# A graph network stack whose run checks its own lists: the check moved beside layer 3, d added by VectorE, ln_b added earlier, and VectorE counted at 0.9 by the planner

## The chip, the cores and the metric

The kernel runs on one core of one Trainium2 chip. The metric is device time in microseconds, as the median of several runs; lower is better. A core has TensorE (PE in the profile; PEld is its weight load), VectorE (DVE), ScalarE (ACT), GpSimd (POOL) and SyncE (SP). Each engine works through its own queue of instructions in order and waits on semaphores for the others. SP issues the plain DMAs, POOL the gathers (indirect DMAs).

## The reference

4096 nodes with 128 features, and a dense 4096 x 4096 adjacency `adj` of which few entries are not zero. There are four layers, each with `h = relu(layernorm(x))` and `x = x + layer(h, adj)`:

```python
# layer 0: h @ W_self.T + (adj @ h) @ W_neigh.T + b
# layer 1: Chebyshev terms: h @ w0 + (adj @ h) @ w1 + (2 * adj @ (adj @ h) - h) @ w2 + bias
# layer 2: attention over the columns of adj, weights exp(leaky_relu(src + dst)) times adj, normalised
# layer 3:
s = node_feats @ msg_w[:, :D].T
d = node_feats @ msg_w[:, D:].T
messages = gelu(s[:, None, :] + d[None, :, :] + msg_b)
aggregated = einsum('ijd,ij->id', messages, adj)
new_feats = concatenate([node_feats, aggregated], -1) @ upd_w.T + upd_b
h = gelu(new_feats) + node_feats
return (h - mean(h)) / sqrt(var(h) + eps) * ln_w + ln_b
```

Only pairs (i, j) with a nonzero entry of `adj` need a message in layer 3.

## The kernel before

The nodes are reordered by their expected degree, which is fixed at build time. The kernel scans `adj` once and builds lists on the chip: of the columns that each stripe of 256 rows needs, and of the single entries of each block of 128 rows. The lengths of all lists are fixed beforehand from the expected degrees with a margin. In the end the kernel looks whether a list has overflowed: `n_bad` is the number of partitions with an overflow. It is loaded into a register of every engine (L1648), and `tc.If(some_bad > 0)` (L1655) runs a dense version, which these inputs never need.

**Stages.** The scan with layer 0 lies between 0 and about 410 us of the profiled span, layers 1 and 2 of the products (both multiplications of the Chebyshev layer) up to about 870, attention up to about 1185, and layer 3 behind it, its start beside the last columns of attention.

**The planner.** The order of all instructions is made while the program is built, by the class `Plan` (L255). Each piece of work is a generator that yields what it wants next: an engine with a duration, a buffer of a pool (`Slots`), or an `Event`. The planner keeps a clock for each engine and serves the piece that can begin first, a lower rank before a higher one within a short patience. What a piece emits after its turn is appended to the program; `in_order` (L348) fixes that order on each engine. So durations that the planner books don't change an instruction, they change the order in which all are issued. `on_dve(n)` books 0.16 + 1.05e-3 n us for VectorE, and PE durations are multiplied by `PE_TIME` (0.72). Where the plan has a gap on PE, `fill` (L604) emits matmuls on a tile of zeros (L609) into an idle bank.

**Layer 3** is the class `Messages` (L1316). It works in eight groups of four blocks of rows. There are 158 chunks of up to 128 list entries, taken in 49 batches of up to four. `d` lies in DRAM (`d_tab`, written at L1307). For each group:

- `prepare` (L1354) computes s for its rows, adds `msg_b` (L1369), makes the diagonal's messages (`own`: add at L1374, GELU at L1376, times the diagonal `r` of L1380, into the accumulator at L1385).
- `message` (L1391), one for each batch: ACT and VectorE build a selection matrix (`mt` at L622, `msel` at L624); VectorE builds `r`, which places the entries' values (L1400); POOL has gathered the rows of `d` into `m` (L553); PE adds in PSUM `ident` times `m` (L1406) and the selected rows of s (L1408); ACT takes the GELU from PSUM back into `m` (L1412); PE multiplies into the accumulator (L1418). The buffers of `m` are four own tiles and halves of attention's e and tau tiles, hence those names in the profile.
- `finish` (L1425) copies the accumulator (L1430), multiplies by the update weights (L597), adds `upd_b` (L1438), GELU (L1441), adds h and takes the mean (L1444 to L1446), squares (L1450), square root (L1453), reciprocal (L1455, L1456), normalises (L1459), multiplies by ln_w (L1463), adds ln_b (L1464) and x (L1465), and stores (L1467).

PSUM has three accumulators, three banks and two "picks", which become banks in layer 3. There are one, later four, lanes for selections and two, later four, tiles `r`. [...]

**The check** (L1621 to L1646) stands after `plan.run()` (L1618), so behind everything on VectorE: 67 comparisons of one element per partition, 12 small operations, one matmul over the partitions (L1644) and a copy to integers (L1646).

Of the kernel before, what the change touches and what calls it, by code (L numbers as in the profile page):

```python
# [254 lines left out]
class Plan:  # L255
# [8 lines left out]
    BYTES = 330e3  # L264
    TABLE = 1.3
    PATIENCE = 0.3
    PE_TIME = 0.72
    FILLED = 0.8
    SHORT = 0.8
# [29 lines left out]
    def run(self, until=lambda: False):  # L299
        while self.tasks and not until():  # L300
            able = []
            for task in list(self.tasks):
                while isinstance(task.want, Event) and task.want.time is not None:
                    if task.want.time + self.HOP > task.ready:
                        task.ready, task.engine = max(task.ready, task.want.time), None
                    self._next(task)
                want = task.want
                if want is None or isinstance(want, Event):
                    continue
                if isinstance(want, Slots):  # L310
                    if not want.free:
                        continue
                    begin = max(task.ready, min(want.free)[0])
                else:
                    begin = max(task.ready + self.HOP * (task.engine != want[0]), self.free[want[0]])
                able.append((begin, task.rank, task.serial, task))
            assert able, [(t.generator.__name__, t.want) for t in self.tasks]
            first = min(able)
            want = first[3].want
            if not isinstance(want, Slots):  # L320

                first = min((a[1:] for a in able if a[0] <= first[0] + min(self.PATIENCE, want[1]) and
                             not isinstance(a[3].want, Slots) and a[3].want[0] == want[0]))
                first = next(a for a in able if a[3] is first[2])
            begin, task = first[0], first[3]
            want = task.want
            if isinstance(want, Slots):
                first = min(want.free)
                want.free.remove(first)
                task.ready = begin  # L330
                self._next(task, want.items[first[1]])
                continue
            duration = want[1]
            if want[0] == "PE":
                duration *= self.PE_TIME
                gap = begin - self.free["PE"]
                if self.filler and gap > self.SHORT:
                    self.filler(self.free["PE"], gap * self.FILLED)
            self.finish = begin + duration
            if len(want) > 2 and want[2] != self.table:  # L340
                self.table = want[2]
                self.finish += self.TABLE
            self.free[want[0]] = self.finish
            task.ready, task.engine = self.finish, want[0]
            self._next(task)
# [33 lines left out]
def sparse_stack(tc, x, adj, adjT, diag, w_self, w_neigh, b0, w1, b1, w2, att_src, att_dst,  # L379
# [10 lines left out]
    with ExitStack() as ctx:  # L390
# [21 lines left out]
        def by_block(v, n):  # L412

            return v[:, None, :].to_broadcast([P, n, D])
# [188 lines left out]

        def fill(begin, time):  # L604

            idle = min((free, i, slots.items) for slots in (banks, picks) for free, i in slots.free + [(1e9, 0)])
            if idle[0] < begin - 1.0:
                for _ in range(int(time / 0.22)):
                    nc.tensor.matmul(idle[2][idle[1]], nothing[:, :P], nothing, start=True, stop=True)  # L609
# [706 lines left out]
        class Messages:  # L1316
# [37 lines left out]
            def prepare(self, g):  # L1354
# [32 lines left out]
                plan.release(owns, own)  # L1387
                plan.release(r_tiles, r)
                self.s_here[g].set(plan.finish)

            def message(self, g, b, u, c, chunks, m, here):  # L1391
                n = len(chunks)
                yield u_done[u.number]
                lane = yield m_lanes
                yield from selection(lane, mids[:, u.number, :], half[:, u.number:u.number + 1], c, n)
                yield self.s_here[g]
                r = yield r_tiles
                yield "DVE", 0.35 * n
                for q, k in enumerate(chunks):
                    nc.vector.tensor_scalar(r[:, q, :], iota_row[:, :P], e_row[:, k:k + 1], e_val[:, k:k + 1],  # L1400
                                            op0=ALU.is_equal, op1=ALU.mult)
                for q in range(n):
                    yield here[q]
                p = yield banks
                yield "PE", n * 0.84
                nc.tensor.matmul(p[:, :n * D], ident, m[:, :n, :], start=True, stop=False)  # L1406
                for q in range(n):
                    nc.tensor.matmul(p[:, q * D:(q + 1) * D], lane["sel"][:, q, :], self.s_rows[g][:, b % GB, :],  # L1408
                                     start=False, stop=q == n - 1)
                plan.release(m_lanes, lane)  # L1410
                yield on_act(n * D, "gelu")
                nc.scalar.activation(m[:, :n, :], rows_of(p, n), AF.Gelu)  # L1412
                plan.release(banks, p)
                yield "PE", 0.42 * n
                acc = self.acc[g]
                for q in range(n):
                    self.left[b] -= 1
                    nc.tensor.matmul(acc[:, b % GB * P:(b % GB + 1) * P], m[:, q, :], r[:, q, :], start=False,  # L1418
                                     stop=all(self.left[g * GB + k] == 0 for k in range(GB)))
                plan.release(r_tiles, r)  # L1420
                plan.release(messages, m)
                if all(self.left[g * GB + k] == 0 for k in range(GB)):
                    plan.start(self.finish(g), -2)

            def finish(self, g):  # L1425
# [33 lines left out]
                    nc.scalar.activation(f[:, k, :], f[:, k, :], AF.Identity, scale=st[:, 2, k:k + 1],  # L1459
                                         bias=st[:, 3, k:k + 1])  # L1460
                plan.release(stats, st)
                yield "DVE", 2.1
                nc.vector.tensor_mul(f, f, by_block(ln_w_sb, GB))  # L1463
                nc.vector.tensor_add(f, f, by_block(ln_b_sb, GB))  # L1464
                nc.vector.tensor_add(f, f, xN[:, blocks, :])  # L1465
                yield SP
                nc.sync.dma_start(out_rows[:, blocks, :], f)  # L1467
# [18 lines left out]
            plan.release(banks, p)  # L1486

        w02, w22, w2T, dst_w = (kept(k, (P, D)) for k in ("w02", "w22", "w2T", "dst_w"))


        making = ctx.enter_context(ExitStack())
# [112 lines left out]
        with tc.tile_pool(name="lm", bufs=1, reuse_waits="tile") as lm:  # L1604
# [10 lines left out]
            more_of(m_lanes, message_lanes(lm, range(1, 4)))  # L1615
            more_of(banks, [picks.items[i] for _, i in picks.free])
            picks.free = []
            plan.run()  # L1618


            bad = lm.tile([P, NPAIR + NU + 2], F32, name="bad", tag="bad")  # L1621
            for i, item in enumerate(ROWS + COLS):
                nc.vector.tensor_scalar(bad[:, i:i + 1], pair_total[:, i:i + 1], float(item.cap * P), None, op0=ALU.is_gt)
            for i, u in enumerate(UNITS):
                nc.vector.tensor_scalar(bad[:, NPAIR + i:NPAIR + i + 1], total[:, i:i + 1], float(u.places), None,
                                        op0=ALU.is_gt)
            nc.vector.tensor_reduce(bad[:, NPAIR + NU:NPAIR + NU + 1], over, axis=AX.X, op=ALU.max)

            count = lm.tile([P, NB], F32, name="count", tag="count")
            found = lm.tile([P, NB], F32, name="found", tag="found")  # L1630
            hub = sum(u.block == 0 for u in UNITS)
            nc.vector.tensor_reduce(count, marks.rearrange("p (b h) -> p b h", h=2), axis=AX.X, op=ALU.add)
            nc.vector.tensor_scalar(count, count, 2.0, float(-N), op0=ALU.mult, op1=ALU.add)
            nc.vector.tensor_scalar(found, diag_sb, 0.0, None, op0=ALU.is_gt)
            nc.vector.tensor_sub(count, count, found)
            nc.vector.tensor_reduce(found[:, 0:1], deg[:, :hub], axis=AX.X, op=ALU.add)
            nc.vector.tensor_copy(found[:, 1:], deg[:, hub:])
            nc.vector.tensor_tensor(count, count, found, op=ALU.not_equal)
            nc.vector.tensor_reduce(bad[:, NPAIR + NU + 1:], count, axis=AX.X, op=ALU.max)
            worst = lm.tile([P, 2], F32, name="worst", tag="worst")  # L1640
            nc.vector.tensor_reduce(worst[:, 0:1], bad, axis=AX.X, op=ALU.max)
            nc.vector.tensor_scalar(worst[:, 1:2], worst[:, 0:1], 0.0, None, op0=ALU.is_gt)
            p = accs.items[0]
            nc.tensor.matmul(p[:, :1], ones, worst[:, 1:2], start=True, stop=True)  # L1644
            n_bad = kept("n_bad", (P, 1), I32)
            nc.vector.tensor_copy(n_bad, p[:, :1])  # L1646
        in_order(tc)
        return nc.values_load(n_bad[0:1, 0:1], min_val=0, max_val=P)  # L1648

# [337 lines left out]
```

## Time and profile before

| what | value |
|---|---|
| runs | 1197.93 us median of three (1197.63, 1197.93, 1202.9) |
| profiled execution | 1500.43 us, of which the span from first to last instruction is 1498.6 us |
| mean granted clock of TensorE | 0.834 |
| gathers of layer 3 (L553 from d_tab) | 158, 0.95 us each, one every 1.25 us |
| ident matmuls of layer 3 (L1406) | 46.2 us busy |
| last store issued (L1467) | 1474.62 us |
| check on VectorE (L1623 to L1646) | 1474.5 to 1481.4 us |

The profiled execution is 302.5 us longer than the median of the runs, so a position in the span is not one in a run. A profile line for an instruction group has line, engine, operation, tiles, count, duration, and the idle time before it with what ended that. "remote" and "another core or an unknown queue" are waits whose end the profile can't name, "issue" is time in which an engine waited for nothing that it shows. Lines of the sequencers (SPq, POOLq and so on) show loads into registers, branches, drains and semaphores, which are not counted as busy.

### The profile page before, as it was taken

Reading aid. Unit: us, or ns where it says so; the run is one execution under the profiler, and the core shown is the slowest. Engines: PE = TensorE matmul, PEld = TensorE weight load, DVE = VectorE, ACT = ScalarE, POOL = GpSimd, SP = SyncE. Lnnn points to the kernel's source line nnn. Section 1 sums busy time; section 2 is a strip of 40 time slices with the busy share of each in tenths; the row PEclk is TensorE's granted clock in tenths of the full one; section 3 lists DMA queues with packets and bytes.
Section 4 is the critical chain, followed back from the end, with each engine's and each line's share of the span. In section 5 each row is a group of like instructions: output and inputs, shape, how many; then the busy total and the mean of one; then the engine's idle time right before and its main releaser. Section 6 shows DMA issues by size and latency. Waiting matters only on the chain.

```text
span 1498.6 us, 19187 instructions
## 1 busy us (share of the span) xinstructions
PE 1058.5 (71%) x5943; PEld 723.0 (48%) x5943; DVE 791.5 (53%) x2982; ACT 670.3 (45%) x1344; POOL 767.3 (51%) x832
## 2 busy tenths in 40 slices
PE   6786788887477867467774289668777955668880
PEld 3454555554256556355653255334444633556660
DVE  5796666886366566355663156334343612344453
ACT  5983666663121212114452087546564801236462
POOL 4135754544455656635667527726576165654500
PEclk9897898888697888677897599879897986888885
DMA  8999999994366778666542045313333121121200
GB/s 252 352 338 318 335 308 342 341 310 145 92 194 191 205 217 232 171 193 176 156 132 80 22 123 146 108 39 87 107 101 97 41 59 43 47 51 48 67 17 17
DMA packets 175415, 236.03 MB, mean 157 GB/s; under 512 B 22452, under 2 KB 155336, under 8 KB 167112
## 3 DMA queue, kind: packets, MB, share of 16 engines
q1 hardware_dynamic: 148904, 186.45, 37.6%
q0 software_dynamic: 26400, 48.27, 13.1%
q8 instruction: 49, 0.80, 0.2%
q14 instruction: 62, 0.51, 0.1%
HBM read 203.41 MB, written 31.23 MB: 157 GB/s over the span
## 4 chain that ended last, share of the span: by engine, by line
PE 26%; issue 11%; ACT 9%; another core or an unknown queue 8%; DVE 5%; DMA 1%; SPq 0%; ACTq 0%; DVEq 0%
PE acc L1254 4%; PE acc L1252 4%; PE bank L597 3%; PE acc L1138 3%; PE acc L1155 2%; PE acc L1418 2%; PE pick L609 1%; PE bank L1406 1%; PE bank L1408 1%; ACT e L1228 1%; ACT junk L1450 1%; ACT e L1231 1%; ACT junk L568 1%; PE pick L1418 1%
## 5 line engine op out<-in xcount | busy, mean ns | idle before, releaser
L553 POOL DMA_INDIRECT e_val<-in_adj,e_at x158 | 155.5, 984 | 48.0 <-issue 46.5
L553 POOL DMA_INDIRECT g<-h_tab,fetch_row x136 | 135.7, 998 | 73.1 <-issue 34.3
L609 PE MATMUL pick<-nothing 128*128 128x512 f16 x532 | 141.4, 413 | 2.4 <-issue 2.4
L1138 PE MATMUL acc<-big,hA 128*128 128x256 f32 x448 | 124.6, 422 | 16.3 <-DMA big<-in_adjT 7.3
L609 PEld LDWEIGHTS <-nothing 128*128 128x128 f16 x795 | 83.5, 108 | 102.7 <-issue 38.3
L553 POOL DMA_INDIRECT g<-a_tab,fetch_col x74 | 77.7, 1049 | 92.5 <-issue 43.6
L553 POOL DMA_INDIRECT rseg<-in_adjT,seg_row x68 | 71.3, 1048 | 94.3 <-issue 39.7
L1138 PEld LDWEIGHTS acc<-big,hA 128*128 128x128 f32 x448 | 90.6, 213 | 32.8 <-DMA big<-in_adjT 8.8
L553 POOL DMA_INDIRECT cseg<-in_adj,seg_col x74 | 70.8, 957 | 66.2 <-DVE pcum L634 23.5
L553 POOL DMA_INDIRECT g<-u_tab,fetch_row x68 | 64.7, 951 | 63.7 <-PE acc L1155 32.5
L890 DVE SCALAR_TENSOR_TENSOR ehit<-ehit,pos,pick 128x32 f32<-128x32 f32 (+7 forms) x158 | 38.8, 285 | 108.0 <-issue 64.6
L1235 DVE TENSOR_TENSOR tau<-e,big 128x512 f32<-128x512 f32 (+3 forms) x61 | 54.2, 889 | 70.2 <-ACT e L1231 43.7
L887 ACT COPY ehit<-pick 128x192 f32<-128x192 f32 (+7 forms) x74 | 20.4, 286 | 157.8 <-remote 72.5
L553 POOL DMA_INDIRECT tau<-d_tab,e_col x63 | 60.5, 961 | 56.2 <-PE acc L1418 15.1
L553 POOL DMA_INDIRECT m<-d_tab,e_col x70 | 68.0, 972 | 38.0 <-issue 16.5
L768 ACT ACTIVATE mask<-dst 128x2048 fp8e4<-128x2048 f32 x43 | 81.8, 1903 | 12.1 <-DMA dst<-in_adj 9.5
L1155 PE MATMUL acc<-big,g 128*128 128x256 f32 x272 | 80.8, 437 | 2.7 <-DMA big<-r_tab 1.9
L622 ACT ACTIVATE sel_t<-iota_row,mids 128x512 f32<-128x512 f32 (+3 forms) x43 | 27.1, 642 | 118.1 <-DVE mids L617 69.8
L568 ACT ACTIVATE junk<-xN,stat 128x128 f32<-128x128 f32 x128 | 51.4, 401 | 60.7 <-DVE stat L564 23.1
L609 PE MATMUL bank<-nothing 128*128 128x512 f16 x263 | 74.8, 430 | 1.6 <-DVE s L1369 1.2
L883 PE MATMUL pick<-eA,esel 128*128 128x65 f16 (+7 forms) x158 | 27.3, 249 | 61.4 <-DVE esel L624 24.1
L1138 PE MATMUL acc<-big,hB 128*128 128x256 f32 x224 | 64.2, 428 | 0.0
(328 smaller groups left out, 2727.5 us busy)
## 6 DMA issues: line engine op xcount, KB each, us to landing
dst<-in_adj SPq DMA_DIRECT2D x43, 1024.0 KB
big<-in_adjT SPq DMA_DIRECT2D x45, 512.0 KB
raw<-in_adj SPq DMA_DIRECT2D x21, 1024.0 KB
big<-in_adjT SPq DMA_DIRECT2D x66, 256.0 KB
big<-r_tab SPq DMA_DIRECT2D x30, 512.0 KB
c_tab<-cseg SPq DMA_DIRECT2D x74, 128.0 KB
r_tab<-rseg SPq DMA_DIRECT2D x68, 128.0 KB
big<-c_tab SPq DMA_DIRECT2D x15, 512.0 KB
```

The costliest lines, as they stand in the source:

```text
L553: nc.gpsimd.indirect_dma_start(out=dst, out_offset=None, in_=table[:, :], in_offset=bass.IndirectOffsetOnAxis(ap=index, axis=0))
L568: nc.scalar.activation(junk, src[:, k, :], AF.Square, bias=st[:, 0, k:k + 1], accum_out=st[:, 1, k:k + 1])
L597: nc.tensor.matmul(p[:, k * D:(k + 1) * D], lhs[:, k * P:(k + 1) * P], w, start=i == 0, stop=i == len(terms) - 1)
L609: nc.tensor.matmul(idle[2][idle[1]], nothing[:, :P], nothing, start=True, stop=True)
L768: nc.scalar.activation(mask[:, h * HALF:(h + 1) * HALF], raw_of[b, h], AF.Sigmoid, scale=1e38, accum_out=marks[:, 2 * b + h:2 * b + h + 1] ...
L890: nc.vector.scalar_tensor_tensor(hit[:, q, :], hit[:, q, :], pos0[:, k + q:k + q + 1], pv[:, q, W:2 * W], op0=ALU.is_le, op1=ALU.mult, acc ...
L1138: nc.tensor.matmul(acc, self.near[:, b, :D], as_rows(t)[:, k, :], start=count == 0, stop=count == every - 1)
L1155: nc.tensor.matmul(acc, row[:, :D], r, start=count == 0, stop=count == every - 1)
L1235: nc.vector.tensor_mul(tau[:, :n, :], e[:, :n, :], a[:, :n, :])
L1252: nc.tensor.matmul(acc[0:1, CS:2 * CS], parts[k][:, D + 1:], tau[:, k, :], start=False, stop=False)
L1254: nc.tensor.matmul(acc[:, :CS], parts[k][:, :D], e[:, k, :], start=False, stop=self.count[s.index] == every - 1)
L1418: nc.tensor.matmul(acc[:, b % GB * P:(b % GB + 1) * P], m[:, q, :], r[:, q, :], start=False, stop=all(self.left[g * GB + k] == 0 for k in ...
```

## The change

Four things are changed.

1. The check becomes a piece of work `missing` for the planner, with the last rank (9), started beside layer 3. It takes a bank for its matmul. In the resulting order it stands at the beginning of layer 3 on VectorE.
2. In `message` PE only makes the selected sums of s, before the gather is waited for; VectorE adds `d` from `m` and the bank into `m` (L1417 of the changed file), the bank is given back, and ACT takes the GELU in place (L1420).
3. ln_b is added to x in `prepare` (L1395), behind the diagonal's matmuls, and no longer in `finish`.
4. The planner multiplies what it books for VectorE by `DVE_TIME` = 0.9. With it the order of all engines changes in all stages. SP's DMAs are moved by 1.5 of 497 places on average, at most 13; the gathers keep their sequence but for the additions on POOL among them.

A key for `min` in `fill` only settles ties.

```diff
 class Plan:
+    DVE_TIME = 0.9
     PE_TIME = 0.72
...
             duration = want[1]
+            if want[0] == "DVE":
+                duration *= self.DVE_TIME
...
             def prepare(self, g):
...
                 self.s_here[g].set(plan.finish)
+                yield on_dve(BANK)
+                nc.vector.tensor_add(xN[:, blocks, :], xN[:, blocks, :], by_block(ln_b_sb, GB))
...
             def message(self, g, b, u, c, chunks, m, here):
...
+                p = yield banks
+                yield "PE", n * 0.42
+                for q in range(n):
+                    nc.tensor.matmul(p[:, q * D:(q + 1) * D], lane["sel"][:, q, :], self.s_rows[g][:, b % GB, :],
+                                     start=True, stop=True)
+                plan.release(m_lanes, lane)
                 for q in range(n):
                     yield here[q]
-                p = yield banks
-                yield "PE", n * 0.84
-                nc.tensor.matmul(p[:, :n * D], ident, m[:, :n, :], start=True, stop=False)
-                for q in range(n):
-                    nc.tensor.matmul(p[:, q * D:(q + 1) * D], lane["sel"][:, q, :], self.s_rows[g][:, b % GB, :],
-                                     start=False, stop=q == n - 1)
-                plan.release(m_lanes, lane)
+                yield on_dve(n * D)
+                nc.vector.tensor_add(m[:, :n, :], m[:, :n, :], rows_of(p, n))
+                plan.release(banks, p)
                 yield on_act(n * D, "gelu")
-                nc.scalar.activation(m[:, :n, :], rows_of(p, n), AF.Gelu)
-                plan.release(banks, p)
+                nc.scalar.activation(m[:, :n, :], m[:, :n, :], AF.Gelu)
...
             def finish(self, g):
...
-                yield "DVE", 2.1
+                yield "DVE", 1.4
                 nc.vector.tensor_mul(f, f, by_block(ln_w_sb, GB))
-                nc.vector.tensor_add(f, f, by_block(ln_b_sb, GB))
                 nc.vector.tensor_add(f, f, xN[:, blocks, :])
...
+        def missing():
+
+            bad = lm.tile([P, NPAIR + NU + 2], F32, name="bad", tag="bad")
+            limits = [(pair_total[:, i:i + 1], float(item.cap * P)) for i, item in enumerate(ROWS + COLS)]
+            limits += [(total[:, i:i + 1], float(u.places)) for i, u in enumerate(UNITS)]
+            for i, (have, most) in enumerate(limits):
+                if i % 8 == 0:
+                    yield "DVE", 0.5
+                nc.vector.tensor_scalar(bad[:, i:i + 1], have, most, None, op0=ALU.is_gt)
...
+            p = yield banks
+            yield on_pe(2)
+            nc.tensor.matmul(p[:, :1], ones, worst[:, 1:2], start=True, stop=True)
+            yield "DVE", 0.2
+            nc.vector.tensor_copy(n_bad, p[:, :1])
+            plan.release(banks, p)
...
+            n_bad = kept("n_bad", (P, 1), I32)
+            plan.start(missing(), 9)
             plan.run()
-
-
-            bad = lm.tile([P, NPAIR + NU + 2], F32, name="bad", tag="bad")
...
-            nc.vector.tensor_copy(n_bad, p[:, :1])
         in_order(tc)
```

More of the change, by code (lines that the diff above doesn't have):

```diff
@@ L604, in fill @@
         def fill(begin, time):
-            idle = min((free, i, slots.items) for slots in (banks, picks) for free, i in slots.free + [(1e9, 0)])
+            idle = min(((free, i, slots.items) for slots in (banks, picks) for free, i in slots.free + [(1e9, 0)]),
+                       key=lambda slot: slot[:2])
             if idle[0] < begin - 1.0:
@@ L1488, in sparse_stack @@
         w02, w22, w2T, dst_w = (kept(k, (P, D)) for k in ("w02", "w22", "w2T", "dst_w"))
+        def missing():
[6 more added lines that the diff above has]
+                nc.vector.tensor_scalar(bad[:, i:i + 1], have, most, None, op0=ALU.is_gt)
+            yield "DVE", 0.5
+            nc.vector.tensor_reduce(bad[:, NPAIR + NU:NPAIR + NU + 1], over, axis=AX.X, op=ALU.max)
+            count = lm.tile([P, NB], F32, name="count", tag="count")
+            found = lm.tile([P, NB], F32, name="found", tag="found")
+            hub = sum(u.block == 0 for u in UNITS)
+            nc.vector.tensor_reduce(count, marks.rearrange("p (b h) -> p b h", h=2), axis=AX.X, op=ALU.add)
+            nc.vector.tensor_scalar(count, count, 2.0, float(-N), op0=ALU.mult, op1=ALU.add)
+            yield "DVE", 0.6
+            nc.vector.tensor_scalar(found, diag_sb, 0.0, None, op0=ALU.is_gt)
+            nc.vector.tensor_sub(count, count, found)
+            nc.vector.tensor_reduce(found[:, 0:1], deg[:, :hub], axis=AX.X, op=ALU.add)
+            nc.vector.tensor_copy(found[:, 1:], deg[:, hub:])
+            yield "DVE", 0.9
+            nc.vector.tensor_tensor(count, count, found, op=ALU.not_equal)
+            nc.vector.tensor_reduce(bad[:, NPAIR + NU + 1:], count, axis=AX.X, op=ALU.max)
+            worst = lm.tile([P, 2], F32, name="worst", tag="worst")
+            nc.vector.tensor_reduce(worst[:, 0:1], bad, axis=AX.X, op=ALU.max)
+            nc.vector.tensor_scalar(worst[:, 1:2], worst[:, 0:1], 0.0, None, op0=ALU.is_gt)
+            p = yield banks
[4 more added lines that the diff above has]
+            plan.release(banks, p)
         making = ctx.enter_context(ExitStack())
@@ L1617, in sparse_stack @@
             picks.free = []
+            n_bad = kept("n_bad", (P, 1), I32)
+            plan.start(missing(), 9)
             plan.run()
-            bad = lm.tile([P, NPAIR + NU + 2], F32, name="bad", tag="bad")
[L1622 to L1645, printed above, removed]
-            nc.vector.tensor_copy(n_bad, p[:, :1])
         in_order(tc)
```

## The prediction

> **What bounds the kernel now.** I read the page's busy shares first, then the chain of work that ended last, then the stretches of layer 3 and of the end, and last the single instructions of the final 25 us.
>
> ```profile
> PE 1058.5 (71%) x5943; PEld 723.0 (48%) x5943; DVE 791.5 (53%) x2982; ACT 670.3 (45%) x1344; POOL 767.3 (51%) x832
> PE 26%; issue 11%; ACT 9%; another core or an unknown queue 8%; DVE 5%; DMA 1%; SPq 0%; ACTq 0%; DVEq 0%
> ```
>
> No engine is full: the kernel is bound by a chain that hops between engines. 19% of that chain (285 us) is time for which the profile names no cause. The profiled execution took 1500.43 us (span 1498.6, 1.8 beside it), the median of the runs is 1197.93: 302.5 us less. I take it that most of the unnamed time belongs to profiling, and carry differences worked out from named instructions over to the median unscaled. That is a choice.
>
> The last stretches, each line giving length, busy time of PE, PEld, DVE, ACT, POOL, then clock and DMA:
>
> ```profile
> 1440.00:1474.60 34.60, 19.32 (x141) 16.74 (x139) 17.11 (x41) 25.36 (x59) 0.00 (x0) 0.85 0.05 16
> 1474.60:1481.40 6.80, 0.58 (x2) 0.50 (x2) 5.85 (x79) 0.00 (x0) 0.00 (x0) 0.50 0.13 40
> 1481.40:1498.60 17.20, 0.00 (x0) 0.00 (x0) 0.00 (x0) 0.00 (x0) 0.00 (x0) 0.50 0.02 6
> ```
>
> After the last useful VectorE operation 6.8 us go to the check of the lists on VectorE alone, and then 17.2 us to nothing that computes. What those 17.2 us are is seen in the lines of the load of n_bad, of the If and of the program's end (duration min/median/max in ns, first and last start):
>
> ```profile
> L1648 POOLq TENSOR_LOAD <-n_bad x1: 497/497/497, 1481.4 to 1481.4; - x1
> ...
> L1655 SPq COMPARE_BRANCH  x1: 50/50/50, 1482.2 to 1482.2; - x1
> ...
> L1655 POOLq INC_SWDGE_SEM  x1: 2500/2500/2500, 1485.8 to 1485.8; - x1
> ...
> L1982 POOLq DRAIN  x3: 46/103/9460, 1488.3 to 1498.4; - x3
> L1982 SPq DRAIN  x3: 7/7/7, 1489.0 to 1498.1; - x3
> ```
>
> All engines load n_bad at 1481.4. POOL then branches, spends 2.5 us on its DMA semaphores and 9.46 us in a drain that ends at 1497.8; SP and the others were through by 1489.0 and wait for it. POOL's last gather was at 1423.3, so it stood idle for 58 us before it could begin this.
>
> [...]
>
> **The change, part by part.**
>
> *Check beside layer 3.* 79 VectorE instructions (5.85 us busy, 6.8 with gaps) and one matmul leave the end. In the changed order they stand on VectorE among the r and msel of the first list batches, about the end of attention, and n_bad is written before layer 3's group 1. So each engine can load n_bad when its own work is done, POOL after its last gather some 50 us before the end: branch, 2.5 and 9.46 us fall beside the last finishes. What is left after the last f: SP's DMA issue (0.43), SP from branch to its drain (1482.2 to 1489.0, 6.8), the last barrier (1497.8 to 1498.6, 0.8): 8.0 us in place of 24.0. The output's DMA, issued at 1474.6, has its own landing inside SP's 6.8. Gain 16.0. Lower bound: if POOL's drain for some reason starts only with the others, the gain is the check and its load, 7.3 + 0.7 = 8.
>
> Its cost where it goes: 24 of the 79 stand ahead of attention's last column sums on VectorE, the other 55 behind them. 24 x 0.06 = 1.5 us come before the last d table, for which POOL waits:
>
> ```profile
> POOL tau L553 <- DMA d_tab<-agg: 12.5, 1, 12.5
> ```
>
> I count 1.5 in full (between 0 and 6.8). The remaining 55 are hidden by VectorE's idleness while POOL streams gathers: 2.9 us busy of the 52 from 1202 to 1254. If that cover were gone they would cost up to 5.
>
> *ln_b ahead.* Eight adds of 692 ns move from finish to prepare. On the chain only the last one counts: 0.7 gained (0.73 from start to start). In prepare it stands behind the diagonal's r, where only later r wait for it; VectorE waits 13.9 us in these groups for ACT's L1459 (bounds 0 to 8 x 0.7 lost; I take 0).
>
> *d by VectorE.* 49 fp32 matmuls with ident (46.2 us busy; on the PE queue 0.64 us for 384 columns, 0.86 for 512) go[...]. The gather's wait moves with it from PE to VectorE. A batch's chain was gather, ident, sums (0.67 to 0.9), gelu; it becomes gather, add, gelu, with the sums ahead. Where gathers are late this saves up to a microsecond a batch[...]. GELU from SBUF costs 630 ns (L1441) against 600 from PSUM: 0.03 each, dropped. What I count: (a) in the last stretch PE is on the chain with two ident pairs (1.28 and 0.65): 1.9 gained. (b) In each of six groups the update matmuls stand behind an ident and sums pair, and the accumulator's copy is through before:
>
> ```profile
> 1389.58 0.81 PE L1406 MATMUL pick<-tau,ident 128*128 128x384 f32 x2
> 1389.78 0.59 ACT L1430 COPY agg<-acc 128x512 f32<-128x512 f32 x1 [2.15 <-PE acc L1418]
> 1390.22 0.83 PE L1408 MATMUL pick<-s,msel 128*128 128x128 f32 x6
> ...
> 1390.89 0.39 PE L597 MATMUL bank<-upd_h_sb,hT 128*128 128x128 f32 x2
> ```
>
> The copy ends at 1390.37, L597 starts at 1390.89: 0.5 x 6 = 3.0 gained. Bounds for the part: 15 us gained (L1406 is 1% of the chain), 20 lost (rival D).
>
> *0.9 in the order.* It makes no instruction faster, it moves them. The plan books an add of 512 at 0.70 us and from now at 0.63, while it takes 0.69; it books r at 0.35 a piece, from now 0.32, while they follow at 0.28. Wide operations become too short in the plan, small ones less too long. Engines behind a wide one will be planned early and wait at the head of their queue. [...] One consequence can be priced: at the end. Before, the last batch's gelu stood on ACT ahead of the last-but-one finish:
>
> ```profile
> 1457.60 0.28 ACT L1412 ACTIVATE e<-bank 128x128 f32<-128x128 f32 x1
> ...
> 1463.00 1.28 ACT L1441 ACT_TABLE_LOAD   x1
> 1464.29 0.63 ACT L1441 ACTIVATE f<-f 128x512 f32<-128x512 f32 x1
> ```
>
> In the changed order it stands behind that finish's Sqrt and the table load. Where at 1464.29 the last f's gelu ran, the last batch's gelu (0.28) will run, then its matmuls (0.5), the copy (0.6), the updates (1458.68 to 1460.96, 2.3), the add with its hop (0.9): 4.6 lost (0 if PE's relief brings the last-but-one finish forward by as much). For the order of the other layers I take 0 and 1% either way (12 us), since neither the scan (DMA 0.91 to 0.93 busy to 340 us) nor POOL's sequence changes much.
>
> **Sum:** 1500.4 - 16.0 - 0.7 + 1.5 - 1.9 - 3.0 + 4.6 = 1484.9, 15.5 below; on the median 1197.9 - 15.5 = 1182.4, said as 1183.
>
> **Rivals.** About 0.5% (6 us) is what a measurement of this kernel can tell from no change.
> A, the forecast: 1176 to 1190, chance 0.53.
> B, the drain is long only under the profiler, or isn't hidden: the end gives 8, the rest loses nothing on balance (1.5 + 4.6 - 1.9 - 3.0 - 0.7 = 0.5): 1190. [...] Against: 9.46 us is one instruction of POOL, and POOL's idle time was long. Chance 0.18, half of it within 0.5% with the order's noise.
> C, layer 3 gains as a whole: the 15 us of ident on the chain go and adds are hidden: 1170. For it: POOL's waits for L1418 to free a buffer (13.5, 7.7 and 6.5 us after 1340). Against: the adds cost nearly as much. Chance 0.14.
> D, slower: a batch now takes its PSUM bank before its gather has landed and keeps it until the add. With four r tiles up to four of five banks stand waiting, and a finish (L597) or prepare that needs one waits for a batch of gathers, 4 x 1.25 = 5.0 us. In seven groups 35 us lost, 15.5 gained: 1217. It decides from 15.5 / 7 = 2.2 us a group. For it: the wait "here" now stands behind "yield banks". Against: PE's order of L597 against the sums of the next group is much as before. Chance 0.10.
> E, the order loses what the end gives: the 12 us of 1% and the 4.6 of the last batch: 1198. Chance 0.05.
>
> **Numbers.** Faster by over 0.5% are A, C and half of B: 0.53 + 0.14 + 0.09 = 0.76. Within it are half of B, most of E: 0.13. Slower 0.11. The range 1166 to 1199 takes A, B, C and E nearly whole and leaves out D.
>
> **What would show it.** In the changed profile POOL's long drain ends before the last f; nothing on VectorE follows the last add to f but the load; the end comes about 8 us after it. No ident matmul is in the list[...]. The last batch's gelu follows a table load. Wrong it would be if the drain still ends the program, if L597 starts wait for DMA or VectorE for over 2 us in each group, or if the stages before layer 3 move by more than 12 us.

## The result, and the profile after

The changed kernel takes 1198.76 us (median of 20 runs, 1188.45 to 1202.36), the kernel before 1196.45 us (20 runs): ratio 1.0004, 95% interval [0.9986, 1.0021]. A second set (e6) gave 1.0020 [1.0001, 1.0039]. So the change is worth nothing, or costs up to 0.4%, where 1183 was forecast.

One thing must be known to read what follows: the profile of before that the prediction used was taken where engines often stand still after the work that they wait for is done (up to 27.9 us at one copy in e1, below), and there the same program takes about 1500 us with or without a profile (1497 and 1505 in e1). Below this is called late releases. The runs of the result (1196 and 1199 us), and the profile of the changed kernel (span 1198.6), are free of it. So the kernel before was profiled once more under the conditions of the result (run f1). The head of its page, with busy shares and the chain of work that ended last:

```profile
span 1192.2 us, 19187 instructions
...
PE 983.1 (82%) x5943; PEld 675.2 (57%) x5943; DVE 793.8 (67%) x2982; ACT 671.9 (56%) x1344; POOL 769.6 (65%) x832
...
PE 29%; DMA 25%; DVE 15%; ACT 12%; POOL 9%; issue 9%; SPq 0%; POOLq 0%; DVEq 0%; ACTq 0%
```

The same lines of the changed kernel:

```profile
span 1198.6 us, 19084 instructions
...
PE 978.6 (82%) x5841; PEld 676.8 (56%) x5841; DVE 817.8 (68%) x3031; ACT 674.5 (56%) x1344; POOL 778.2 (65%) x832
...
PE 25%; DVE 24%; DMA 22%; ACT 14%; POOL 8%; issue 8%; SPq 0%; DVEq 0%; POOLq 0%; ACTq 0%
```

"Another core or an unknown queue" is gone from both chains, and DMA has 22 to 25% of them instead of 1%. VectorE has 49 instructions more (3031 against 2982): the 49 adds of d, 0.55 us each for 384 columns and 0.69 for 512, 28.5 in all. Its share of the chain goes from 15 to 24%.

**The end came as forecast, and a little better.** The changed kernel's lines of the last add on VectorE (time line: start, duration), and of n_bad's load, the If and the program's end (duration min/median/max in ns, first and last start):

```profile
1192.04 0.69 DVE L1471 TENSOR_TENSOR f<-f,xN 128x512 f32<-128x512 f32 x1
```

```profile
L1663 POOLq TENSOR_LOAD <-n_bad x1: 506/506/506, 1155.1 to 1155.1; - x1
...
L1670 POOLq INC_SWDGE_SEM  x1: 2500/2500/2500, 1165.2 to 1165.2; - x1
...
L1670 SPq COMPARE_BRANCH  x1: 50/50/50, 1193.2 to 1193.2; - x1
...
L1997 POOLq DRAIN  x3: 46/103/9460, 1167.8 to 1198.3; - x3
L1997 SPq DRAIN  x3: 7/7/7, 1197.7 to 1198.0; - x3
```

POOL's semaphores (2.5 us) and its drain of 9.46 us now begin at 1165.2 and 1167.8, beside the last finishes, while VectorE works until 1192.73. In f1 everything still follows the last add, which ends at 1167.9:

```profile
L1655 POOLq INC_SWDGE_SEM  x1: 2500/2500/2500, 1179.4 to 1179.4; - x1
...
L1982 POOLq DRAIN  x3: 46/103/9460, 1181.9 to 1191.9; - x3
L1982 SPq DRAIN  x3: 7/7/7, 1182.5 to 1191.6; - x3
```

From the issue of the last store to the end of the span it is 5.8 us where it was 24.2. These 18.4 us are real, and they are lost elsewhere.

**Where they are lost: one gate and one stream.** The last table of d is stored by SP, and POOL gathers from it. The lines of that store and of POOL's next gather, f1 first:

```profile
L1307 SPq DMA_DIRECT2D d_tab<-agg x8: 360/414/1093, 782.8 to 964.4; - x8
```

```profile
967.28 0.94 POOL L553 DMA_INDIRECT tau<-d_tab,e_col  x1 [10.79 <-DMA d_tab<-agg]
968.53 0.95 POOL L553 DMA_INDIRECT tau<-d_tab,e_col  x1 [0.30 <-issue]
```

and in the changed kernel:

```profile
L1311 SPq DMA_DIRECT2D d_tab<-agg x8: 360/367/462, 788.3 to 983.3; - x8
```

```profile
971.50 0.93 POOL L556 DMA_INDIRECT e<-d_tab,e_col  x1 [0.30 <-issue]
986.24 1.08 POOL L556 DMA_INDIRECT e<-d_tab,e_col  x1 [13.81 <-DVE msel L628]
```

In both POOL stands idle (10.8 and 13.8 us) until 2.9 us after the last store to d_tab is issued; the profile names VectorE in the second case, but the gather starts 2.9 us after that store in each of the ten profiles of the table. Then it issues the remaining 137 of the 158 gathers with never a gap of 1 us. Counted from the traces, this divides every kernel's end into four pieces (us; scan and last d_tab store are times from the start of the span, the next three columns are lengths; scan: end of the last mask; the two rows of the changed kernel are the profile of the result and that of run e6):

| kernel | scan | last d_tab store | to the end of the last gather | to the last store of out | to the end | span |
|---|---|---|---|---|---|---|
| before (f1) | 312.3 | 964.4 | 178.0 | 25.6 | 24.2 | 1192.2 |
| check alone (f2) | 309.9 | 965.6 | 178.3 | 29.3 | 5.8 | 1179.0 |
| check behind d (h4) | 312.0 | 966.2 | 177.6 | 25.6 | 5.8 | 1175.2 |
| all at 1.0 (f3) | 316.1 | 976.6 | 179.2 | 22.3 | 5.8 | 1183.9 |
| all, 0.9 late (h2) | 312.2 | 975.7 | 178.9 | 32.1 | 5.8 | 1192.5 |
| 0.9 alone (f4) | 318.9 | 972.1 | 177.3 | 38.5 | 24.1 | 1212.0 |
| all, 0.9 early (h1) | 322.4 | 991.0 | 178.9 | 22.6 | 5.7 | 1198.2 |
| changed kernel | 320.1 | 983.3 | 179.5 | 30.0 | 5.8 | 1198.6 |
| changed kernel (e6) | 319.2 | 977.7 | 177.5 | 30.9 | 5.8 | 1191.9 |
| check, 1.1 (h3) | 314.8 | 992.4 | 178.1 | 26.1 | 5.9 | 1202.5 |

The third piece is the same everywhere, 177.3 to 179.5. The changed kernel (e6) loses 13.3 us ahead of the last d_tab store and 5.3 behind the last gather, and gains 18.4 at the end: -0.3 together, as the spans say (1191.9 against 1192.2). The profile of the result has +18.9 in the first piece. Single profiles of one kernel differ by some 5 us there (983.3 and 977.7), and that of h1 is the longest of its 22 runs (1200.0, median 1191.0), so the sizes of the parts are taken from timed ratios below, and the places from this table.

### The profile page after: what moved, and what is told of

The parts are those of the page before. It is cut to its first block, busy times and chain, and to the rows that moved or that the text cites. A ratio compares the mean times of both kernels' runs of the same rounds, so it can differ in the third digit from the quotient of the medians.

```text
span 1198.6 us, 19084 instructions
## 1 busy us (share of the span) xinstructions
PE 978.6 (82%) x5841; PEld 676.8 (56%) x5841; DVE 817.8 (68%) x3031; ACT 674.5 (56%) x1344; POOL 778.2 (65%) x832
## 4 chain that ended last, share of the span: by engine, by line
PE 25%; DVE 24%; DMA 22%; ACT 14%; POOL 8%; issue 8%; SPq 0%; DVEq 0%; POOLq 0%; ACTq 0%
POOL e_val L556 5%; DMA e_val<-in_adj,e_at 4%; ACT mask L772 4%; DMA dst<-in_adj 4%; PE bank L600 3%; PE acc L1159 3%; PE pick L613 3%; PE acc L1142 3%; PE acc L1256 3%; DMA cseg<-in_adj,seg_col 2%; PE acc L1258 2%; DMA g<-a_tab,fetch_col 2%; ACT junk L571 2%; DMA big<-r_tab 2%; DMA tau<-d_tab,e_col 2%
## 5 line engine op out<-in xcount | busy, mean ns | idle before, releaser
L556 POOL DMA_INDIRECT e_val<-in_adj,e_at x158 | 167.2, 1058 | 48.0 <-issue 41.9
L613 PE MATMUL pick<-nothing 128*128 128x512 f16 x574 | 152.2, 414 | 0.0
L1142 PE MATMUL acc<-big,hA 128*128 128x256 f32 x448 | 120.7, 413 | 14.5 <-DMA big<-in_adjT 9.8
L556 POOL DMA_INDIRECT rseg<-in_adjT,seg_row x68 | 68.7, 1010 | 62.9 <-issue 37.2
L1159 PE MATMUL acc<-big,g 128*128 128x256 f32 x272 | 75.6, 415 | 7.2 <-DMA big<-r_tab 5.8
L556 POOL DMA_INDIRECT tau<-d_tab,e_col x65 | 64.0, 985 | 19.8 <-issue 10.7
L1159 PEld LDWEIGHTS acc<-big,g 128*128 128x128 f32 x272 | 53.8, 208 | 18.9 <-DMA cseg<-in_adj,seg_col 6.2
L1142 PE MATMUL acc<-big,hB 128*128 128x256 f32 x224 | 59.7, 408 | 5.7 <-DMA big<-in_adjT 5.7
L891 ACT COPY ehit<-pick 128x192 f32<-128x192 f32 (+9 forms) x74 | 20.4, 288 | 76.2 <-PE pick L888 68.8
L983 POOL TENSOR_TENSOR xN<-xN,b_sb 128x1024 f32<-128x1024 f32 x4 | 10.8, 2701 | 69.7 <-ACT hA L581 52.1
```

The costliest lines, as they stand in the source:

```text
L556: nc.gpsimd.indirect_dma_start(out=dst, out_offset=None, in_=table[:, :], in_offset=bass.IndirectOffsetOnAxis(ap=index, axis=0))
L1142: nc.tensor.matmul(acc, self.near[:, b, :D], as_rows(t)[:, k, :], start=count == 0, stop=count == every - 1)
L1159: nc.tensor.matmul(acc, row[:, :D], r, start=count == 0, stop=count == every - 1)
```

## The experiments

The theory: the order planned with 0.9 loses what the end gains. Its rivals: d by VectorE loses it in layer 3, or the gain at the end isn't real.

### The kernel before again, e1, e5 and f1

No edit.

> The kernel before, unchanged, for a profile without the 302 us that had no name. Theory 1 (the gain at the end is real and was lost elsewhere): span 1190 to 1200, from the last add to f on VectorE to the end still about 24 us, of these some 9.5 in POOL's drain; so the last add ends at about 1172, and in the changed kernel (1192.7) about 20 us later: the loss is then seen as stages that end later. Rival (the drain is long only in a stretched profile): under 14 us from the last add to the end, and the stages of layer 3 within 8 us of the changed kernel's.

> The kernel before, unchanged. In the run of e1 semaphore events came up to 35 us after the end of the instruction that gives them, and the program took 1497 us with and 1505 without a profile; in the run of the changed kernel they came within 2 us. If that belongs to the chip or the hour and not to the program, this run, in the condition of the 1196 us, shows no such delay, and a span of 1190 to 1200; then 24 us from the last add to f to the end (theory 1), or under 14 (the drain is long only with late semaphores). If it belongs to the program, it is 1495 again.

> The kernel before, for its stages where it takes about 1196 us. Theory 1 (the gain at the end is real, the order lost it): the last add to f ends at about 1172 and 24 us follow, so the stages of the changed kernel end some 20 us later than these, most of it ahead of layer 3. Rival 1 (the end is short here too): under 14 us after the last add; then layer 3 and all before it agree within 8 us with the changed kernel. Where semaphores come late: 1495 to 1550 again.

e1 took 1497 us beside 1505 for the runs without a profile, e5 1551 beside 1552: it is not profiling that stretches the program. The spans of 1190 to 1200 that were expected came only with f1, which took 1194 us. Some of the longest waits of e1 (us in total, times, longest), and its time line at ScalarE's longest wait of the kind "issue":

```profile
POOL g L553 <- issue: 89.9, 212, 25.6
...
PE bank L597 <- issue: 71.4, 19, 40.4
...
ACT tau L1412 <- remote: 46.6, 2, 35.3
```

```profile
814.66 0.19 PE L883 MATMUL pick<-eA,esel 128*128 128x65 f16 x1
...
822.22 0.17 ACT L1041 ACTIVATE hB<-bank 128x2 f32<-128x2 f32 x1 [10.96 <-issue]
...
850.26 0.24 ACT L887 COPY ehit<-pick 128x96 f32<-128x96 f32 x1 [27.87 <-issue]
```

The copy waits for semaphores of PE and VectorE. PE had made its input by 814.9 and nothing on VectorE ran between 822.9 and 850.5, yet the copy starts at 850.26. In f1 the first of the three groups reads

```profile
POOL g L553 <- issue: 53.6, 177, 0.3
```

with a longest wait of 0.3 in place of 25.6. From the end of each VectorE instruction that gives a semaphore to the first event of that semaphore after it, 97 in 100 came within 0.01 us in f1 and within about 7 us in e1 (ScalarE 13, TensorE 8). In the changed kernel's profile it is 0.01 us again, in the prediction's of before 5.7 (ScalarE 11, TensorE 6). The figures of e1 and of the prediction's profile are upper bounds, because e1's record has fewer events at all (1321 for VectorE's 1941 instructions), and a missing one makes the next look late. Slower matmuls alone don't account for it: PE's busy time is 83 us longer in e1 than in f1 (1066.5 and 983.1), the span 303. Why releases come late is open. What it did to the prediction: in e1 POOL's stream has gaps (35.0 us put down to L1418 among them) and takes 221 us for the 137 gathers that f1 does in 175, so the profile showed no stream at all. The end after the last add is 24 us in f1 too, so the rival that the drain is long only in a stretched profile has fallen.

### The check alone, e2 and f2

`missing` replaces the lines behind `plan.run()`, everything else as before:

```diff
-            plan.run()
-            bad = lm.tile([P, NPAIR + NU + 2], F32, name="bad", tag="bad")
...
+            n_bad = kept("n_bad", (P, 1), I32)
+            plan.start(missing(), 9)
+            plan.run()
```

> Only the check of the lists moves beside layer 3; message, finish, prepare and the planner's 1.0 stay as before. Theory 1 (its gain is real): 0.985 to 0.990 of before (12 to 18 us less). Rival (drain long only in a stretched profile, or the check costs in front of layer 3 what the end gives): 0.996 to 1.002.

> Only the check moves. In the condition with late semaphores it took 23 us less (e2). Theory 1: 0.985 to 0.990 here too, 12 to 18 us. Rival 1 (the drain is long only with late semaphores, or what precedes layer 3 pays): 0.997 to 1.002.

e2: 0.9845 [0.9768, 0.9921]. f2: 1178.76 us against 1195.45, 0.9841 [0.9797, 0.9885]. The check's move alone is worth 16.7 us between the medians. Its profile, of a run 2.3 us over its median, has 18.4 gained at the end, and 1.2 lost ahead of d_tab (965.6 against 964.4), 0.3 in the stream and 3.7 in the tail (the stretch from the last gather to the last store of out), where its order differs from that of before.

### All but 0.9, e3 and f3

```diff
-    DVE_TIME = 0.9
+    DVE_TIME = 1.0
```

> The changed kernel with DVE_TIME = 1.0, so the check, ln_b and d by VectorE are in it and the order is planned as before. Theory 1a (the order from 0.9 lost about 15 us): 0.984 to 0.991. Theory 1b (d by VectorE lost it in layer 3): 0.996 to 1.004, as with 0.9.

> The changed kernel with DVE_TIME = 1.0. Theory 1a (the order lost about 16 us): 0.984 to 0.991. Theory 1b (d by VectorE lost it in layer 3): 0.996 to 1.004.

e3: 0.9892 [0.9827, 0.9958]. f3: 1182.78 us, 0.9883 [0.9843, 0.9922]. Without 0.9 the change is worth 12.7 us between the medians. So 0.9 is what takes it.

### 0.9 alone, e4 and f4

The kernel before with `DVE_TIME = 0.9`, the lines that multiply by it, and the key that settles ties in `fill`.

> The kernel before with DVE_TIME = 0.9 in the planner and nothing else. Theory 1a (the order lost about 15 us): 1.008 to 1.016. Theory 1b (d by VectorE lost it): 0.997 to 1.003.

> The kernel before with DVE_TIME = 0.9 alone. Theory 1a: 1.008 to 1.016 (with late semaphores it was 1.035). Theory 1b: 0.997 to 1.003.

e4: 1.0347 [1.0261, 1.0433]. f4: 1216.05 us, 1.0163 [1.0114, 1.0213]. Nothing that computes is added or changed, only the order, the fill and the choice of buffers, and it costs 20 us. Of these, f4's row of the table has 7.7 ahead of the last d_tab store and 12.9 in the tail. Theory 1b falls; theory 1a stands, with a loss just above its range in f4 and, where releases come late, of twice its range in e4.

### The changed kernel again, e6

> The changed kernel, unchanged, beside the kernel before. Where before takes about 1196 us: 1.000 again. Where semaphore events come late and before takes 1500 to 1550: theory 1 adds the parts measured on such a chip: -1.1% for all but the order (e3), +3.5% for the order (e4), so 1.02 to 1.03. Rival (the parts don't add, a late semaphore costs whatever is on the path): 0.99 to 1.01, as in the other condition.

1.0020 [1.0001, 1.0039], with before at 1196.62: the result again, if anything 0.2% slower. There were no late releases here, so what the changed kernel does with them wasn't measured.

### 0.9 early or late, g1, g2, h1 and h2

The planner runs in several calls; the constant is switched ahead of the last one, behind the end of attention.

```diff
     # early
+            plan.DVE_TIME = 1.0
             plan.start(missing(), 9)
     # late, with DVE_TIME = 1.0 in the class
+            plan.DVE_TIME = 0.9
             plan.start(missing(), 9)
```

> The changed kernel, but the planner goes back to 1.0 where the last plan begins (behind the end of attention), so 0.9 orders only scan, products and attention. Theory (both parts lose, about 7 us early and 9 at the end): 0.993 to 0.998 of before, 1190 us. Rival 1 (all is lost early): 1.000 to 1.004. Rival 2 (all is lost at the end): 0.986 to 0.990, as f3.

> The reverse: 1.0 until the end of attention, 0.9 only in the last plan (layer 3 but for its beginning). Theory (both lose): 0.994 to 0.998, with the last store about 31 us after the last gather. Rival 1 (all is lost early): 0.986 to 0.990. Rival 2 (all at the end): 1.000 to 1.004.

> 0.9 until the end of attention, 1.0 in the last plan. Where before takes about 1196 us: theory (about 7 us early and 9 at the end) 0.993 to 0.998; rival 1 (all early) 1.000 to 1.004; rival 2 (all at the end) 0.986 to 0.990. With late semaphores 1.015 to 1.02 as in g1.

> 1.0 until the end of attention, 0.9 in the last plan. Where before takes about 1196 us: theory 0.994 to 0.998, last store about 31 us after the last gather; rival 1 0.986 to 0.990; rival 2 1.000 to 1.004. With late semaphores about 1.00 as in g2.

g1 and g2 ran with late releases: 1.0177 [1.0075, 1.0278] and 1.0013 [0.9967, 1.0058], both above what was expected. h1: 1190.97 us, 0.9960 [0.9943, 0.9977]. h2: 1190.81 us, 0.9936 [0.9914, 0.9958], just under the theory's range. Against f3's 0.9883, 0.9 costs 0.77% (9.2 us) early and 0.53% (6.3 us) late; by the intervals each is good to about 5 us. The sum 0.9883 + 0.0077 + 0.0053 = 1.0013 lies inside both intervals of the changed kernel. Counted back from the changed kernel (1.0004 and 1.0020) instead, the early part is 0.68 to 0.84% and the late one 0.44 to 0.60%. Both rivals (all early, all late) fall.

Early: the table shows the scan ending at 319 to 322 in the four profiles with 0.9 there, and at 310 to 316 in the five with 1.0 (f3 and h2, which share the order up to there, at 316.1 and 312.2). Lines of the last mask on ScalarE, f1 and f4:

```profile
L768 ACT ACTIVATE mask<-dst x43: 1892/1910/1911, 28.7 to 310.4; 128x2048 fp8e4<-128x2048 f32 x43
```

```profile
L772 ACT ACTIVATE mask<-dst x43: 1892/1910/1914, 28.7 to 317.0; 128x2048 fp8e4<-128x2048 f32 x43
```

Each mask takes as long as before (1910 ns); the last starts 6.6 us later. By the traces the 17th of the 21 loads of `raw` is issued at 255 to 256 us with 0.9 (f4, h1, e6) and at 244 to 245 with 1.0 (f1, f2, h2). From 225 to 258 us SP's DMAs of that line wait 19.7 us in all for ScalarE's masks in f4 and 12.9 in f1. Which moved instruction is behind it stays open, and so does the rest of the early loss.

Late: it is the last batch. ScalarE's time line in f1, and then in the changed kernel, at the last-but-one finish:

```profile
1150.37 0.63 ACT L1441 ACTIVATE f<-f 128x512 f32<-128x512 f32 x1 [2.34 <-DVE f L1438]
1150.98 0.28 ACT L1412 ACTIVATE e<-bank 128x128 f32<-128x128 f32 x1
...
1154.77 1.28 ACT L1453 ACT_TABLE_LOAD   x1
...
1157.67 0.63 ACT L1441 ACTIVATE f<-f 128x512 f32<-128x512 f32 x1
```

```profile
1170.82 0.63 ACT L1448 ACTIVATE f<-f 128x512 f32<-128x512 f32 x1 [2.64 <-DVE f L1445]
...
1175.33 1.28 ACT L1460 ACT_TABLE_LOAD   x1
...
1176.94 1.28 ACT L1420 ACT_TABLE_LOAD   x1
1178.23 0.31 ACT L1420 ACTIVATE e<-e 128x128 f32<-128x128 f32 x1
...
1183.19 0.63 ACT L1448 ACTIVATE f<-f 128x512 f32<-128x512 f32 x1 [2.64 <-DVE f L1445]
```

The last batch's GELU (128x128) follows the finish's GELU at once in f1; in the changed kernel it stands behind the square root and two table loads. From layer 3's first GELU on, one table load (`ACT_TABLE_LOAD`, 1.28 us) stands at each change of ScalarE between GELU and square root (17 each in the prediction's profile of before and in the changed kernel). From the last-but-one finish's GELU to the last one it is 7.31 us in f1, and also in f3 and h1, which have d on VectorE but 1.0 in the last plan; it is 12.37 in the changed kernel and in h2. So these 5.1 us belong to 0.9 and not to d on VectorE.

A rival for both parts is TensorE's granted clock, which also differs: as means of the runs 0.910 for the changed kernel in e6, 0.909 and 0.917 for h1 and h2, 0.926 and 0.927 for before beside them. It doesn't sort the times. f3 and h2 have 0.916 and 0.917 and differ by 0.53%; h3 (below) is slower than the changed kernel at 0.929. Over the first 320 us the changed kernel's two profiles show 0.90, as f1, f3 and h2 do, and end the scan 3 to 8 us later. (f4 and h1 show 0.88 there, so in them the clock may add to it.)

### Check and one more part, g3 and g4

g3 adds ln_b in `prepare`, g4 the new `message`, each to the check alone at 1.0.

> Check moved and ln_b added in prepare, order at 1.0, message as before. If ln_b is worth what the prediction gave it: 0.983 to 0.985 (0.7 us under f2). Rival (the add in prepare costs the 4 us between f2 and f3): 0.987 to 0.990.

> Check moved and d added by VectorE, order at 1.0, ln_b as before. If d by VectorE costs the 4 us between f2 and f3: 0.987 to 0.990. Rival (ln_b costs it, d by VectorE is worth 0 to 5): 0.980 to 0.985.

g3: 0.9872 [0.9757, 0.9988]. g4: 0.9896 [0.9863, 0.9930]. Both ran with late releases, beside e2's 0.9845 [0.9768, 0.9921] and e3's 0.9892 [0.9827, 0.9958]. g4 falls where the theory had it and outside the rival's range, but its interval meets that of e2, and g3's is too wide to say anything. By the ratios it stays open which of the two costs the 4.0 us between f2 and f3, and those 4.0 us are themselves near the noise: the intervals of f2 and f3 overlap, though each run of f3 is longer than five of the six of f2. f3's lower clock (0.916 against 0.934) could be part of it.

The traces say more. The last two stores of d_tab, in g3 and in g4 (time line of SP):

```profile
1177.45 0.37 SPq L1308 DMA_DIRECT2D d_tab<-agg  x1
...
1198.50 0.36 SPq L1308 DMA_DIRECT2D d_tab<-agg  x1
```

```profile
1185.58 0.37 SPq L1308 DMA_DIRECT2D d_tab<-agg  x1
...
1210.86 0.36 SPq L1308 DMA_DIRECT2D d_tab<-agg  x1
```

Between them lie 21.1 us in g3, as in e2, and 25.3 in g4. All nine profiles with d on VectorE have 24.1 to 26.2 there, the eleven without it 19.5 to 23.0, with late releases or not. So just ahead of the gate d on VectorE costs 2 to 4 us, and ln_b nothing that can be seen. Part of it may be the granted clock, which in this stretch is 0.73 to 0.89 in the nine and 0.92 to 1.0 in the eleven; which causes which isn't shown. The check's 24 comparisons cost about 2 there: 21.9 in f2, 19.9 in f1, and 20.0 in h4 (below), where they stand behind.

The table says where ln_b and d on VectorE together cost and gain: the tail is 22.3 to 22.6 instead of 25.6 (f3, h1), while the last d_tab store comes at 975.7 to 976.6 instead of 964.4 to 966.2. In f3 the chain to that store is crowded on VectorE (time line):

```profile
959.83 1.53 DVE L1504 TENSOR_SCALAR bad<-pair_total 128x1 f32<-128x1 f32 x24
961.29 0.80 DVE L628 TENSOR_SCALAR msel<-mt,half 128x384 f32<-128x384 f32 x2
962.01 0.15 DVE L1287 RECIPROCAL stat<-bank 128x2 f32<-128x2 f32 x1
```

The reciprocal opens the last columns' path to d_tab. 24 comparisons and two selections stand ahead of it, and ScalarE waits 4.55 us for what follows. The comparisons' 1.53 us are the 1.5 of the prediction. Of the 10 us about 5 lie between the last two stores (24.8 in f3, 24.1 in h2, 19.9 in f1); the others build up over the stores before, and what makes them is open.

### Another constant, and the check held back, h3 and h4

```diff
     # h3: the check alone, and
+    DVE_TIME = 1.1
     # h4: the check alone, and in missing, whose event is made ahead
+            yield last.s_here[2]
```

> The check alone is moved, and the planner counts VectorE at 1.1. Theory 2 (the plan at 1.0 fits best, a change either way costs): 0.990 to 1.000. Rival (0.9 costs because it books wide operations too short; 1.1 books them long and is no worse): 0.980 to 0.986, as f2 or under.

> The check alone is moved and waits for the third group's s, so it stands behind the last d_tab. If its 24 instructions ahead of the d_tab cost 2 to 4 us: 0.980 to 0.983. Rival (they cost nothing): 0.984 to 0.986 as f2. In both the load of n_bad on SP stands ahead of the first store and waits for the check: if that delayed the stores, they would come later than in f2, but the last not.

h3: 1202.39 us, 1.0062 [1.0038, 1.0087], 2.2% over the check alone at 1.0, and slower than even theory 2 had it. The rival falls: booking longer costs too. That is two constants on either side of 1.0, not a curve, and why 1.0 is better than both isn't shown. By the table the loss lies ahead of d_tab (992.4).

h4: 1177.36 us, 0.9843 [0.9819, 0.9868]. In its profile d_tab's last store (966.2) is no earlier than in f2; its tail is f1's again (25.6). By the ratio it is f2's equal: the rival holds, in that the 2 us gained between the last two stores don't show in the whole. f2 and h4 both beat the kernel before and the changed one; of what was tried, the check's move with nothing else has the lowest ratio, with f3's interval overlapping.

## Why the prediction was wrong, point by point

- **The step that failed** is "For the order of the other layers I take 0 and 1% either way (12 us), since neither the scan (DMA 0.91 to 0.93 busy to 340 us) nor POOL's sequence changes much". It put the order at nothing, and its reason didn't hold: with 0.9 the last mask of the scan starts 6.6 us later (f4). The order costs 9.2 us early (h1), which had no term, and 6.3 late (h2), of which the last batch was priced. The size of 1% was about right, but it stood in the range and not in the sum. Together 0.9 loses 15.5 us where everything else gains 12.7 (f3).
- **What came** is near rival E ("the order loses what the end gives"), with its 12 and 4.6 against 9.2 and 6.3 measured, to which I gave 0.05. Its 1198 leaves out the 4.1 us that the other terms gain; with them E is 1194. The range of 1166 to 1199 just takes in 1198.76, because it was drawn to take in E; the forecast itself (A, 0.53) is no nearer for it.
- **"Gain 16.0" at the end**: right in mechanism, 18.4 by the profiles (24.2 to 5.8). POOL's drain lies beside the last finishes; SP needs 4.5 us from branch to drain (1193.2 to 1197.7) in place of the 6.8 I carried over.
- **"1.5 in full" for the check ahead of d_tab**: 1.53 us in f3's trace, and 21.9 (f2) against 19.9 (f1) us between the last two stores of d_tab. Right, though h4 shows that removing it gains nothing that its interval can tell.
- **"4.6 lost" by the last batch**: 12.4 - 7.3 = 5.1 us between the last two finishes' GELUs. Right; it was the one part of the order that had a price.
- **(a) and ln_b, 1.9 + 0.7 gained in the tail**: 25.6 - 22.3 = 3.3 in f3. Right for the tail.
- **(b), 3.0 gained in six groups**: wrong under the conditions of the result. Between the last d_tab store and the last gather every kernel takes 177.3 to 179.5; POOL's stream has no gap of 1 us in which a shorter chain of PE could show. I had read waits of POOL for L1418 in a profile where releases come late, and took them for a bound. Where releases come late the gain is there, and larger: the 137 gathers take 220.0 to 227.8 us in the six profiles without d on VectorE (before, e1, e2, e4, e5, g3) and 208.8 to 217.5 in the four with it (e3, g1, g2, g4). So the profile wasn't misread; it showed a bound that the timed runs don't have.
- **What else had no term**: d by VectorE and ln_b beside attention's last columns. The last d_tab store is about 10 us later in f3 and h2 than in f1, f2 and h4, which eats the tail's 3.3 and more: by the ratios f3 (0.9883) is 0.4% over f2 and h4 (0.9841, 0.9843), with overlapping intervals.
- **Carrying differences over unscaled**: it held for the end (the drain is 9460 ns in both profiles) and for the tail, but not for the order, where 0.9 costs 3.5% with late releases and 1.6% without. That "most of the unnamed time belongs to profiling" is wrong: runs without a profile are as long (1505 us beside e1's 1497).
- **Rivals**: B falls (5.8 us after the last store; f2 gives 0.984). C falls, since layer 3 is POOL's stream, 177.3 to 179.5 us (under late releases C's mechanism shows, see (b)). D falls too: batches hold banks while they wait (42.4 us in all before the adds of d, for gathers, in the changed kernel), but the stream stays at 177.5 to 179.5, so nothing is lost there.
- **The test I named**, stages before layer 3 that move by more than 12 us, came true: 13.3 us (e6) and 18.9 (the profile of the result) at the last d_tab store.

## What to carry to other kernels

If the span of a profile is far from the runs' median, take another before pricing anything: here it showed bounds that the runs don't have. Before pricing a chain, look for a queue that streams without gaps and for what opens it: here 137 gathers in 178 us behind one store, while the stretch between the two took 177.3 to 179.5 us in every kernel of the table. A planner's constant is a change of every stage at once: try it by itself, in both directions, and don't bundle it with an edit whose gain is known. A check that ends in a register and a branch was worth finishing early here (16.7 us, f2): each engine then takes its branch as its own work ends (in the changed kernel POOL at 1155.6 us, ScalarE at 1190.2, VectorE at 1192.7, SP at 1193.2), and POOL's drain of 9.46 us lies beside the others' work.

## What was unexpected of the hardware

The same program took 1195 us on some chips and 1497 to 1552 us on others, with or without a profile. In the long runs engines stand still for up to 41 us without anything in the profile that holds them ("issue", "remote", "another core or an unknown queue"), and the granted clock is lower (0.833 in e1, 0.926 in f1). The worth of an edit differs between the two conditions: 0.9 alone costs 3.5% in one and 1.6% in the other, the check's move gains 1.6% in both.
